# Reordering two stages of a four-layer graph network: deferred message sums in layer 2, blocks turned ahead in the front

## The chip, the cores and the metric

The kernel runs on one core of one Trainium2 chip. Its time is the device time of one launch in microseconds (us); the kernel before took 5975.33 us (median of 3 runs, 5974.05 to 5976.02). The profile comes from one further execution under the profiler, which took 6542.29 us by the clock and 6540.2 us from its first to its last instruction. So the profiled execution is longer than the timed ones, and numbers of the profile are used here to see which work waits for which, and how long single pieces take.

The engines are named as in the profile: PE (matmuls; PEld is its weight load), DVE (vector), ACT (scalar), POOL (which here issues the gathers), SP (which issues the plain DMAs). Each engine runs its own instructions in the order in which the program names them, so the order of the program text inside a loop is itself a tuning choice.

## The reference

Node features `x` are 4096 x 512, there are 65536 edges (`src`, `dst`, sorted by `dst`) with 64 attributes each. Four layers follow, each added to `x` after a layer norm and a relu. Cut to what matters here:

```python
# layer 0: attention. h = x W per head, scores of every edge, softmax over a node's edges
h = jnp.einsum('nc,hcf->hnf', x, W)
s_src = jnp.einsum('hnf,hf->hn', h, a_src); s_dst = jnp.einsum('hnf,hf->hn', h, a_dst)
...                                   # masked softmax over the adjacency, att @ h
# layer 1: agg @ weight, agg a degree-normed sum over edges
...
# layer 2: a message for every edge
edge_feat = jnp.concatenate([x[src], x[dst], edge_attr], axis=-1)
h = mish(edge_feat @ W1 + b1)
messages = mish(h @ W2 + b2)                                   # 65536 x 512
agg = jax.ops.segment_sum(messages, dst, num_segments=x.shape[0])
...                                   # two more products, a layer norm
# layer 3: a degree-normed sum over edges
```

`mish(x)` is `x * tanh(softplus(x))`.

## The kernel before

The edges are sorted on the chip (a bitonic sort of keys) and cut into tiles of 128 edges whose ends lie in one block of 128 nodes. A sum over a node's edges is then a matmul of a tile with a one-hot matrix of its places in the block, added to the accumulator `acc` of that block. Three parts of the kernel are concerned.

**Layer 2, the messages.** It handles 528 tiles in 132 groups of four (`U2 = 4`). The groups are software-pipelined: an iteration `i` does the second product of group `i-1`, the attribute product of group `i+1` and the sums of group `i-2`. A message tile is split into two float32r parts, so that a sum is two matmuls (`add_message`):

```python
def in_parts(m):
    parts = lp.tile([P, 2, 2, D], F32R, name="parts", bufs=2)
    nc.vector.tensor_copy(parts[:, 0], m)
    nc.vector.tensor_sub(parts[:, 1], m, parts[:, 0].bitcast(F32))
    return parts

def add_message(t, oh, parts):
    ps = lps.tile([P, D], F32, name="small_ps", bufs=4)
    for k in range(2):
        nc.tensor.matmul(ps, oh, parts[:, k], start=k == 0, stop=k == 1)
    add_to(block_of(nc.vector, bi_d, t), ps)          # DVE: acc[block] += ps

for i in range(-3, NG + 2):
    ...                                               # gathers of later groups (POOL)
    if now(i - 2):
        oh = one_hots(...)                            # DVE
        ...                                           # sigmoid of z (ACT)
    if now(i - 1):
        ps = second_product(h_t.pop(0))               # PE, 4 matmuls of 128x512
        nc.vector.tensor_add(zz[:, 0, :], ps, b2_bc)
    if now(i + 1):
        et = turn_attributes(...)                     # PE transposes, ACT copy
    if now(i - 1):
        h_t[2], h_t[3] = turn_h(2, hh), turn_h(3, hh)
    ...
    if now(i - 1):
        ps = second_product(h_t.pop(1))
        nc.vector.tensor_add(zz[:, 1, :], ps, b2_bc)
    if now(i + 1):
        made = attribute_products(et)                 # PE, 4
        ...                                           # 4 adds into pg (DVE)
    ...                                               # second_product 2 and 3
        nc.vector.tensor_mul(mz[:, :2], mz[:, :2], t[:, :2]); parts = [in_parts(mz[:, :2])]
    ...
        nc.vector.tensor_mul(mz[:, 2:], mz[:, 2:], t[:, 2:]); parts.append(in_parts(mz[:, 2:]))
    ...
    if now(i):
        for j in range(2): h_t[j] = turn_h(j, last)   # PE transposes, ACT copies
    if now(i - 2):
        for j in range(U2):
            add_message(..., oh[:, j, :], parts[j // 2][:, :, j % 2, :])
```

`parts`, `small_ps`, `tr_ps` (of the transposes) and `m_ps` (of the second product) are rings of 2, 4, 2 and 2 buffers; `oh` and `t` have one.

**The front: the product of layer 0.** For each of 32 blocks of 128 nodes, `project` normalizes (`hn`, DVE), turns (four transposes, PE; copy with relu, ACT), multiplies (four matmuls `wh_ps`, four narrow `s_ps`), and puts the block before away:

```python
for j in range(BG):
    ... # hn (DVE)
    yield
    h_t = relu_t(lp, lps, hn)         # PE transposes into tr, ACT relu to h_t
    if waiting is not None:
        put_away(*waiting)            # ACT copy, DVE copy, DMA to htab
    yield
    ps = lps.tile([P, D], F32, name="wh_ps")
    for k in range(KC):
        nc.tensor.matmul(ps, h_t[:, k, :], w_sb[:, k, :], ...)
        if k == 1: yield
    ... # s_ps: four matmuls of 128x16
    yield
```

Three generators take turns at their `yield`s: `project`, the sort `by_order(0)` (three of its steps to two turns), and `attributes` (DMAs).

**The end of a sort.** `placed` turns the sorted tiles (five groups of up to 128 tiles) so that a tile's edges lie along the partitions. It does so one group at a time through one PSUM buffer named `turn`; for `by_order(0)` it is called three times, for `by_order(1)`, beside the sums of layer 1, once:

```python
for g in range(G):
    n = min(P, TT - g * P)
    ps = ppool.tile([P, P], F32, name="turn")
    nc.tensor.transpose(ps, what[:, g, :], ident)
    nc.vector.tensor_copy(into[:, g * P:g * P + n], ps[:, :n])
```

Of the kernel before, what the change touches and what calls it, by code (L numbers as in the profile page):

```python
# [34 lines left out]
def kernel(  # L35
# [90 lines left out]
    def by_order(o, pool, ppool):  # L126
# [156 lines left out]

        def placed(into, what):

            for g in range(G):
                n = min(P, TT - g * P)
                ps = ppool.tile([P, P], F32, name="turn")
                nc.tensor.transpose(ps, what[:, g, :], ident)
                nc.vector.tensor_copy(into[:, g * P:g * P + n], ps[:, :n])  # L290

        blk_bc = blk.unsqueeze(2).to_broadcast([P, G, P])
        val = pool.tile([P, G, P], F32, name="val")
        if o == 1:
            nc.vector.scalar_tensor_tensor(val, blk_bc, float(-D_BLOCK), cur, op0=OP.mult, op1=OP.add)
            nc.vector.tensor_scalar(val, val, float(E), None, op0=OP.min)

            nc.vector.tensor_scalar(val, val, float(EA), odd, op0=OP.mult, op1=OP.add)
            yield
            placed(d_eid, val)  # L300
            return
        cur_i = pool.tile([P, G, P], I32, name="cur_i")
        nc.vector.tensor_copy(cur_i, cur)
        low = pool.tile([P, G, P], I32, name="low")
        nc.vector.tensor_scalar(low, cur_i, N - 1, None, op0=OP.bitwise_and)
        nc.vector.tensor_copy(val, low)
        placed(s_dst, val)
        nc.vector.tensor_scalar(cur_i, cur_i, 12, None, op0=OP.logical_shift_right)
        loc = pool.tile([P, G, P], F32, name="loc")
        nc.vector.tensor_copy(loc, cur_i)  # L310
        nc.vector.scalar_tensor_tensor(loc, blk_bc, float(-P), loc, op0=OP.mult, op1=OP.add)
        placed(s_loc, loc)

        new = pool.tile([P, G, P], F32, name="new")
        nc.vector.tensor_tensor(new, cur, prev, op=OP.not_equal)
        nc.vector.tensor_tensor(val, cur_i, low, op=OP.not_equal)
        nc.vector.tensor_mul(new, new, val)
        placed(s_new, new)
        yield

    def attributes(pool):
# [99 lines left out]
    def relu_t(pool, ppool, hn, relu=True):  # L421

        ps = ppool.tile([P, KC, P], F32, name="tr")
        for k in range(KC):
            nc.tensor.transpose(ps[:, k, :], hn[:, k * P:(k + 1) * P], ident)
        h_t = pool.tile([P, KC, P], F32, name="h_t")
        nc.scalar.activation(h_t, ps, AF.Relu if relu else AF.Copy)
        return h_t
# [16 lines left out]
    def one_hots(pool, loc, t0, n, bufs=None, ids=None, dtype=F32):  # L445

        oh = pool.tile([P, n, P], dtype, name="oh", bufs=bufs)
        nc.vector.tensor_tensor(oh, (row_i if ids is None else ids).unsqueeze(1).to_broadcast([P, n, P]),
                                loc[:, t0:t0 + n].unsqueeze(2).to_broadcast([P, n, P]), op=OP.is_equal)
        return oh  # L450
# [31 lines left out]
    def project(lp, lps):  # L482

        xs = {}

        def load(g):
            xs[g] = lp.tile([P, BG, D], F32, name="xt", bufs=3)
            nc.sync.dma_start(xs[g], blocks_of(x, g * BG))

        load(0)  # L490
        w_sb = lp.tile([P, KC, D], F32, name="w_sb", bufs=1)
        for h in range(H):
            nc.sync.dma_start(w_sb[:, :, h * F:(h + 1) * F], w0[h].rearrange("(k p) f -> p k f", p=P))
        wa = lp.tile([P, KC, 2, H], F32, name="wa", bufs=1)

        def weights_of_scores():
            for j in range(2):
                a_bc = lp.tile([P, H, F], F32, name="a_bc")
                nc.sync.dma_start(a_bc, a0[:, j * F:(j + 1) * F, 0].partition_broadcast(P))
                for k in range(KC):  # L500
                    t = lp.tile([P, H, F], F32, name="w_a")
                    nc.vector.tensor_mul(t, w_sb[:, k, :].rearrange("p (h f) -> p h f", h=H), a_bc)
                    nc.vector.reduce_sum(wa[:, k, j, :], t, axis=AX.X)
                    if k % 2:
                        yield

        class Later:


            def __init__(self, g):  # L510
                self.x = xs.pop(g)
                self.st = lp.tile([P, BG, 2], F32, name="st")
                self.rstd = lp.tile([P, BG], F32, name="rstd")
                self.root = lp.tile([P, BG], F32, name="root")

            def steps(self):
                var = self.st[:, :, 1]
                for j in range(BG):
                    stats(lp, self.st[:, j, :], self.x[:, j, :])
                    yield  # L520
                nc.vector.tensor_scalar(var, var, EPS, None, op0=OP.add)
                nc.scalar.activation(self.root, var, AF.Ln)
                nc.scalar.activation(self.rstd, self.root, AF.Exp, scale=-0.5)
                yield
                nc.vector.tensor_mul(self.root, self.rstd, self.rstd)
                nc.vector.tensor_mul(self.root, self.root, var)
                nc.vector.tensor_scalar(self.root, self.root, -0.5, 1.5, op0=OP.mult, op1=OP.add)
                nc.vector.tensor_mul(self.rstd, self.rstd, self.root)
                yield

        def put_away(b, ps, s_ps):
            nc.scalar.copy(acc[:, b, :D], ps)
            nc.vector.tensor_copy(node[:, b, 0:3:2, :], s_ps)
            nc.sync.dma_start(htab[b * P:(b + 1) * P, :D], acc[:, b, :D])

        groups = NB // BG
        norm = Later(0)
        load(1)
        yield from norm.steps()
        waiting = None  # L540
        for g in range(groups):
            if g + 2 < groups:
                load(g + 2)
            nxt = Later(g + 1) if g + 1 < groups else None
            ahead = nxt.steps() if nxt else iter(())
            for j in range(BG):
                hn = lp.tile([P, D], F32, name="hn")
                nc.vector.tensor_scalar(hn, norm.x[:, j, :], norm.st[:, j, 0:1], norm.rstd[:, j:j + 1],
                                        op0=OP.subtract, op1=OP.mult)
                next(ahead, None)  # L550
                yield
                h_t = relu_t(lp, lps, hn)
                if waiting is not None:
                    put_away(*waiting)
                yield
                ps = lps.tile([P, D], F32, name="wh_ps")
                for k in range(KC):
                    nc.tensor.matmul(ps, h_t[:, k, :], w_sb[:, k, :], start=k == 0, stop=k == KC - 1)
                    if k == 1:
                        yield  # L560
                if g == 0 and j == 0:
                    yield from weights_of_scores()
                s_ps = lps.tile([P, 2, H], F32, name="s_ps")
                for k in range(KC):
                    nc.tensor.matmul(s_ps.rearrange("p j h -> p (j h)"), h_t[:, k, :],
                                     wa[:, k].rearrange("p j h -> p (j h)"), start=k == 0, stop=k == KC - 1)
                waiting = g * BG + j, ps, s_ps
                if j % 2:
                    next(ahead, None)
                yield  # L570
            for _ in ahead:
                pass
            norm = nxt
        put_away(*waiting)

    with tc.tile_pool(name="sort", bufs=1) as sp, tc.tile_pool(name="sort_ps", bufs=1, space=PSUM) as spp, \
# [443 lines left out]
    with ExitStack() as l2:  # L1020
# [9 lines left out]
        def messages(ctx, first, last, fetched=None):  # L1030
# [53 lines left out]
            def second_product(h_t):  # L1084
                m_ps = lps.tile([P, D], F32, name="m_ps")
                product(m_ps, h_t, w2_sb)
                return m_ps
# [26 lines left out]


            fetched, rows, h, z, h_t = dict(fetched or {}), {}, {}, {}, {}
            pg = qg = None
            ctx.enter_context(tc.manual_schedule(engines=ENGINES))
            for i in range(-3, NG + 2):
                now = lambda k: 0 <= k < NG  # L1120
                if now(i + 2):
                    rows[i + 2] = fetch_rows(fetched[i + 2])
# [6 lines left out]
                if now(i) and i > 0:  # L1129
                    nc.scalar.activation(qg, qg, AF.Arctan)  # L1130
                if now(i - 2):
                    oh = one_hots(lp, d_loc, first + (i - 2) * U2, U2, bufs=1, dtype=F32R)
                    mz = z.pop(i - 2)
                    t = lp.tile([P, U2, D], F32, name="t", bufs=1)
                    nc.scalar.activation(t, mz, AF.Sigmoid, scale=-1.0)
                if now(i - 1):
                    hh = h.pop(i - 1)
                    zz = z[i - 1] = lp.tile([P, U2, D], F32, name="z", bufs=2)
                    ps = second_product(h_t.pop(0))
                    nc.vector.tensor_add(zz[:, 0, :], ps, b2_bc)  # L1140
                if now(i + 1):
                    et = turn_attributes(fetched[i + 1])
                    nxt = rows[i + 1]
                if now(i - 1):
                    h_t[2], h_t[3] = turn_h(2, hh), turn_h(3, hh)
                if now(i - 2):
                    nc.scalar.activation(t, t, AF.Arctan)
                if now(i + 1):
                    keep_ends(i + 1, fetched.pop(i + 1))
# [31 lines left out]
                    for j in range(2):  # L1181
                        h_t[j] = turn_h(j, last)
                if now(i - 2):
                    for j in range(U2):
                        add_message(first + (i - 2) * U2 + j, oh[:, j, :], parts[j // 2][:, :, j % 2, :])

        with tc.If(nc.values_load(more[:, 1:2], min_val=0, max_val=1) > 0):
            messages(TD_MAIN, TD)
# [220 lines left out]
```

## Time and profile before

| what | us |
|---|---|
| timed runs, median | 5975.33 |
| profiled execution, first to last instruction | 6540.2 |
| PE, DVE, ACT, POOL busy | 5567.4, 4364.9, 3086.2, 3919.6 |
| second product of layer 2: first and last start | 2384.1, 5122.1 |
| message sums of layer 2: first and last start | 2425.3, 5141.3 |
| front: first transpose of `project` | 24.2 |
| front: the last `node` copy of `project` | 265.65 |
| first gather of layer 0's attention | 275.98 |

The busy time of an engine over the whole span mixes stages with different limits; each of the changed stages is a stretch of its own in the trace (the front from 0 to about 270 us, the messages from about 2384 to 5144 us), and is read there. A line of the timeline gives the start, the time covered, the engine, the source line, the operation, what it writes and reads, the shape and the number of merged instructions; square brackets hold the idle time of that engine just before it and what ended it. float32 matmuls appear as two records each.

### The profile page before, as it was taken

The page shows a single profiled execution, that of the slowest core. Times are in us where ns is not written, and L with a number is a line of the kernel's source. Part 1 is how long each engine was busy: PE and PEld are TensorE (multiplying, and loading weights), DVE is VectorE, ACT ScalarE, POOL GpSimd, SP SyncE. Part 2 cuts the span into 40 slices and gives each one's busy share as a digit, 9 for nine tenths or more (in the row PEclk, how much of TensorE's full clock was granted, in tenths as well). Part 3 has the DMA queues.
Part 4 walks back from the last instruction along what each step waited for, and adds up shares of the span by engine and source line. Part 5 has one row for each costly group of instructions (what it writes and reads, how often), then busy time and mean ns, then how long its engine had stood idle before and what let it go on. Part 6 is the DMA issues. An engine that isn't in the chain of part 4 may idle for free. (4 is left out here: it accounts for less than half of the span.)

```text
span 6540.2 us, 65028 instructions
## 1 busy us (share of the span) xinstructions
PE 5567.4 (85%) x17918; PEld 2951.3 (45%) x17918; DVE 4364.9 (67%) x7420; ACT 3086.2 (47%) x4232; POOL 3919.6 (60%) x3326
## 2 busy tenths in 40 slices
PE   6576777688998869999999999999999899777777
PEld 4355555533443334444444444444444566422222
DVE  7466666755665448888888888888888555455555
ACT  3144444431110047777777777777777433100000
POOL 1255555316665658888888888888887111255664
PEclk9788888899999989999999999999999999877878
DMA  8655555456777745555555555555555111355665
GB/s 228 160 151 149 146 152 153 131 179 211 226 226 197 214 106 115 108 108 108 108 110 109 107 107 108 108 108 109 110 108 104 68 68 65 111 163 165 194 197 161
DMA packets 424659, 908.43 MB, mean 139 GB/s; under 512 B 135734, under 2 KB 135734, under 8 KB 424278
## 3 DMA queue, kind: packets, MB, share of 16 engines
q0 software_dynamic: 264768, 721.66, 44.6%
q1 hardware_dynamic: 159510, 182.40, 8.7%
q8 instruction: 153, 2.51, 0.2%
q14 instruction: 228, 1.87, 0.1%
HBM read 800.88 MB, written 102.94 MB: 138 GB/s over the span
## 5 line engine op out<-in xcount | busy, mean ns | idle before, releaser
L442 PE MATMUL m_ps<-w_sb,h_t 128*128 128x512 f32 x4224 | 1894.1, 596 | 3.2 <-ACT h_t L1081 3.0
L847 PE MATMUL sum_ps<-g,oh 128*128 128x512 f32 x2144 | 1152.5, 673 | 286.5 <-DVE acc L463 145.6
L442 PEld LDWEIGHTS m_ps<-w_sb,h_t 128*128 128x128 f32 x4224 | 781.9, 190 | 937.8 <-issue 922.9
L463 DVE TENSOR_TENSOR acc<-acc,sum_ps 128x512 f32 x800 | 550.0, 687 | 796.7 <-PE sum_ps L847 336.2
L1048 POOL DMA_INDIRECT pg<-qtab,eg x528 | 947.1, 1794 | 161.2 <-issue 160.6
L453 POOL DMA_INDIRECT pg<-ptab,eg x528 | 773.8, 1466 | 217.3 <-issue 160.3
L761 PE MATMUL sum_ps<-rows,oh 128*128 128x261 f32 x2176 | 619.3, 440 | 287.5 <-issue 197.6
L847 PEld LDWEIGHTS sum_ps<-g,oh 128*128 128x128 f32 x2144 | 429.1, 212 | 951.4 <-issue 574.1
L453 POOL DMA_INDIRECT g<-ytab,s_dst x544 | 544.7, 1001 | 491.3 <-DMA x_mid<-x 201.0
L453 POOL DMA_INDIRECT rows<-htab,s_dst x544 | 518.1, 952 | 482.1 <-PE sum_ps L761 285.6
L453 POOL DMA_INDIRECT g<-ztab,d_src x528 | 511.6, 969 | 409.5 <-PE sum_ps L847 173.2
L761 PEld LDWEIGHTS sum_ps<-rows,oh 128*128 128x128 f32 x2176 | 453.5, 217 | 391.8 <-issue 203.8
L988 POOL DMA_INDIRECT eg<-aug,d_eid x528 | 517.6, 980 | 160.9 <-issue 142.9
L1081 ACT COPY h_t<-tr_ps 128x512 f32<-128x512 f32 x528 | 296.3, 587 | 292.5 <-PE tr_ps L1079 271.7
L1349 ACT ACTIVATE t_end<-acc,dis 128x512 f32<-128x512 f32 x32 | 23.0, 722 | 847.9 <-DVE acc L463 806.4
L463 DVE TENSOR_TENSOR acc<-acc,small_ps 128x512 f32 x528 | 362.5, 687 | 80.2 <-DVE acc L463 60.6
L1099 PE MATMUL small_ps<-parts,oh 128*128 128x512 f32 x1056 | 314.9, 420 | 91.4 <-DVE parts L1093 80.7
L1156 DVE TENSOR_TENSOR pg<-pg,small_ps 128x512 f32<-128x512 f32 x528 | 328.3, 683 | 66.3 <-issue 38.6
L1152 DVE TENSOR_TENSOR z<-m_ps,b_bc 128x512 f32<-128x512 f32 x132 | 91.3, 692 | 376.7 <-PE m_ps L442 345.8
L1093 DVE TENSOR_TENSOR parts<-z,parts 128x1024 fp32r<-128x1024 f32 x264 | 323.4, 1225 | 9.0
L1079 PE MATMUL tr_ps<-ident,pg 128*128 128x128 f32 x2112 | 302.3, 276 | 5.4 <-DVE pg L1167 2.1
L768 DVE TENSOR_TENSOR acc<-acc,sum_ps 128x522 f32 x272 | 189.5, 697 | 173.7 <-PE sum_ps L761 159.6
(276 smaller groups left out, 8716.9 us busy)
## 6 DMA issues: line engine op xcount, KB each, us to landing
aug<-row SPq DMA_DIRECT2D x32, 560.0 KB
xt<-in_x_dram SPq DMA_DIRECT2D x16, 1024.0 KB
row<-in_edge_attr_dram SPq DMA_DIRECT2D x32, 512.0 KB
rows<-htab,s_dst POOLq DMA_INDIRECT x544
g<-ytab,s_dst POOLq DMA_INDIRECT x544
eg<-aug,d_eid POOLq DMA_INDIRECT x528
pg<-ptab,eg POOLq DMA_INDIRECT x528
pg<-qtab,eg POOLq DMA_INDIRECT x528
```

Of the source, the lines that this page charges most:

```text
L442: nc.tensor.matmul(ps, h_t[:, k, :], w_sb[:, k0 + k, :], start=start and k == 0, stop=stop and k == KC - 1)
L453: nc.gpsimd.indirect_dma_start(out=dst_ap, out_offset=None, in_=table, in_offset=bass.IndirectOffsetOnAxis(ap=idx, axis=0))
L463: nc.vector.tensor_add(into, into, ps)
L761: nc.tensor.matmul(ps[:, c, :HW], oh[:, j + k, :], rows[:, j + k, c * HW:(c + 1) * HW], start=k == 0, stop=k == 1)
L847: nc.tensor.matmul(ps, oh[:, j + k, :], g[:, j + k, :], start=k == 0, stop=k == pair - 1)
L988: nc.gpsimd.indirect_dma_start(out=eg[:, j // 2, (j % 2) * HALF:(j % 2 + 1) * HALF], out_offset=None, in_=aug.rearrange("e c -> (e c)").un ...
L1048: nc.gpsimd.indirect_dma_start(out=pg[:, j, :], out_offset=None, in_=qtab, in_offset=bass.IndirectOffsetOnAxis(ap=end_of(eg, j, 1), axis=0 ...
L1079: nc.tensor.transpose(h_ps[:, k, :], h[:, j, k * P:(k + 1) * P], ident)
L1081: nc.scalar.copy(h_t, h_ps)
L1093: nc.vector.tensor_sub(parts[:, 1], m, parts[:, 0].bitcast(F32))
L1099: nc.tensor.matmul(ps, oh, parts[:, k], start=k == 0, stop=k == 1)
L1156: nc.vector.tensor_add(nxt[:, j], nxt[:, j], made[j])
```

## The change

In layer 2 only the first two of a group's four sums stay at the end of the iteration. The other two are kept in a list `left` and issued in the next iteration, right behind the first `second_product` and ahead of its `zz` addition; the one-hots of the next group move behind them, since `oh` has one buffer. This is meant to give the second `in_parts` of the group time to end before PE comes to the sums that read it. The loop runs one iteration longer, for the last group's two sums.

In the front the normalized blocks come from a generator `norms()`, and the block `b+1` is turned between the two halves of the product of block `b`, so that PE has matmuls to do while ACT copies the turned block. And `placed` turns four groups into one PSUM tile and takes them away with one copy, with a `yield` between the transposes and the copy.

```diff
         def placed(into, what):
-            for g in range(G):
-                n = min(P, TT - g * P)
-                ps = ppool.tile([P, P], F32, name="turn")
-                nc.tensor.transpose(ps, what[:, g, :], ident)
-                nc.vector.tensor_copy(into[:, g * P:g * P + n], ps[:, :n])
+            for g in range(0, G, 4):
+                n = min(4, G - g)
+                ps = ppool.tile([P, n, P], F32, name="turn")
+                for k in range(n):
+                    nc.tensor.transpose(ps[:, k, :], what[:, g + k, :], ident)
+                yield
+                cols = slice(g * P, min((g + n) * P, TT))
+                nc.vector.tensor_copy(into[:, cols], ps.rearrange("p g t -> p (g t)")[:, :cols.stop - cols.start])
 ... (placed(...) becomes yield from placed(...), four times)
 ... (project; norms() makes the hn, with the same steps of the next norm between)
-                h_t = relu_t(lp, lps, hn)
-                if waiting is not None:
-                    put_away(*waiting)
-                yield
-                ps = lps.tile([P, D], F32, name="wh_ps")
-                for k in range(KC):
-                    nc.tensor.matmul(ps, h_t[:, k, :], w_sb[:, k, :], start=k == 0, stop=k == KC - 1)
-                    if k == 1:
-                        yield
+        for b in range(NB):
+            ps = lps.tile([P, D], F32, name="wh_ps")
+            for k in range(KC // 2):
+                nc.tensor.matmul(ps, h_t[:, k, :], w_sb[:, k, :], start=k == 0, stop=False)
+            yield
+            h_next = relu_t(lp, lps, hn) if b + 1 < NB else None
+            if waiting is not None:
+                put_away(*waiting)
+            yield
+            for k in range(KC // 2, KC):
+                nc.tensor.matmul(ps, h_t[:, k, :], w_sb[:, k, :], start=False, stop=k == KC - 1)
+            hn = next(made, None)
+            yield
 ... (the narrow products s_ps as before; then h_t = h_next)
 ... (layer 2)
-            for i in range(-3, NG + 2):
+            for i in range(-3, NG + 3):
 ...
                 if now(i - 2):
-                    oh = one_hots(lp, d_loc, first + (i - 2) * U2, U2, bufs=1, dtype=F32R)
                     mz = z.pop(i - 2)
 ...
                     ps = second_product(h_t.pop(0))
+                while left:
+                    add_message(*left.pop(0))
+                if now(i - 1):
                     nc.vector.tensor_add(zz[:, 0, :], ps, b2_bc)
 ...
                 if now(i - 2):
+                    oh = one_hots(lp, d_loc, first + (i - 2) * U2, U2, bufs=1, dtype=F32R)
                     nc.scalar.activation(t, t, AF.Arctan)
 ...
                 if now(i - 2):
-                    for j in range(U2):
-                        add_message(first + (i - 2) * U2 + j, oh[:, j, :], parts[j // 2][:, :, j % 2, :])
+                    left = [(first + (i - 2) * U2 + j, oh[:, j, :], parts[j // 2][:, :, j % 2, :]) for j in range(U2)]
+                    for j in range(2):
+                        add_message(*left.pop(0))
```

More of the change, by code (lines that the diff above doesn't have):

```diff
@@ L299, in by_order @@
             yield
-            placed(d_eid, val)
+            yield from placed(d_eid, val)
             return
@@ L306, in by_order @@
         nc.vector.tensor_copy(val, low)
-        placed(s_dst, val)
+        yield from placed(s_dst, val)
         nc.vector.tensor_scalar(cur_i, cur_i, 12, None, op0=OP.logical_shift_right)
@@ L311, in by_order @@
         nc.vector.scalar_tensor_tensor(loc, blk_bc, float(-P), loc, op0=OP.mult, op1=OP.add)
-        placed(s_loc, loc)
+        yield from placed(s_loc, loc)
         new = pool.tile([P, G, P], F32, name="new")
@@ L317, in by_order @@
         nc.vector.tensor_mul(new, new, val)
-        placed(s_new, new)
+        yield from placed(s_new, new)
         yield
@@ L534, in put_away @@
             nc.sync.dma_start(htab[b * P:(b + 1) * P, :D], acc[:, b, :D])
[L536 to L539, printed above, removed]
-        waiting = None
[L541 to L550, printed above, removed]
-                yield
-                h_t = relu_t(lp, lps, hn)
-                if waiting is not None:
-                    put_away(*waiting)
-                yield
-                ps = lps.tile([P, D], F32, name="wh_ps")
-                for k in range(KC):
-                    nc.tensor.matmul(ps, h_t[:, k, :], w_sb[:, k, :], start=k == 0, stop=k == KC - 1)
-                    if k == 1:
[L560 to L573, printed above, removed]
@@ new lines, in norms @@
+        def norms():
+            norm = Later(0)
+            load(1)
+            for _ in norm.steps():
+                yield None
+            for g in range(NB // BG):
+                if g + 2 < NB // BG:
+                    load(g + 2)
+                nxt = Later(g + 1) if g + 1 < NB // BG else None
+                ahead = nxt.steps() if nxt else iter(())
+                for j in range(BG):
+                    hn = lp.tile([P, D], F32, name="hn")
+                    nc.vector.tensor_scalar(hn, norm.x[:, j, :], norm.st[:, j, 0:1], norm.rstd[:, j:j + 1],
+                                            op0=OP.subtract, op1=OP.mult)
+                    next(ahead, None)
+                    if j % 2:
+                        next(ahead, None)
+                    yield hn
+                for _ in ahead:
+                    pass
+                norm = nxt
@@ new lines, in project @@
+        made = norms()
+        for hn in made:
+            if hn is not None:
+                break
+            yield
+        h_t = relu_t(lp, lps, hn)
+        hn = next(made)
+        yield
+        waiting = None
+        for b in range(NB):
[6 more added lines that the diff above has]
+                put_away(*waiting)
+            yield
+            for k in range(KC // 2, KC):
+                nc.tensor.matmul(ps, h_t[:, k, :], w_sb[:, k, :], start=False, stop=k == KC - 1)
+            hn = next(made, None)
+            yield
+            if b == 0:
+                yield from weights_of_scores()
+            s_ps = lps.tile([P, 2, H], F32, name="s_ps")
+            for k in range(KC):
+                nc.tensor.matmul(s_ps.rearrange("p j h -> p (j h)"), h_t[:, k, :],
+                                 wa[:, k].rearrange("p j h -> p (j h)"), start=k == 0, stop=k == KC - 1)
+            waiting = b, ps, s_ps
+            h_t = h_next
+            yield
@@ L1116, in messages @@
             fetched, rows, h, z, h_t = dict(fetched or {}), {}, {}, {}, {}
-            pg = qg = None
+            pg, qg, left = None, None, []
             ctx.enter_context(tc.manual_schedule(engines=ENGINES))
-            for i in range(-3, NG + 2):
+            for i in range(-3, NG + 3):
                 now = lambda k: 0 <= k < NG
```

## The prediction

> **What bounds the kernel now.** I read the page's 40 slices first, for the stages, and then each changed stage by itself.
>
> ```profile
> PE   6576777688998869999999999999999899777777
> PEclk9788888899999989999999999999999999877878
> ```
>
> The messages of layer 2 (2384 to 5144 us) are the long row of nines: PE is nearly full there, at full clock. The table of windows says how full:
>
> ```profile
> 3400.00:3900.00 500.00, 484.86 (x1589) 239.56 (x1587) 405.29 (x555) 394.16 (x313) 411.96 (x289) 1.00 0.53 108
> ```
>
> Columns: window; busy time of PE, PEld, DVE, ACT, POOL; granted clock; DMA share; GB/s. PE is idle for 15.1 of 500 us. One group lasts 20.78 us (the record that starts at 3600.58 comes again at 3621.36), so PE idles 15.1 x 20.78 / 500 = 0.63 us a group. The timeline of PE over one group shows where:
>
> ```profile
> 3600.58 1.99 PE L1072 MATMUL small_ps<-w1e,et 64*128 64x512 f32 x8
> 3602.50 7.13 PE L442 MATMUL m_ps<-w_sb,h_t 128*128 128x512 f32 x16
> 3609.47 1.04 PE L1079 MATMUL tr_ps<-ident,pg 128*128 128x128 f32 x8
> 3610.26 1.39 PE L1099 MATMUL small_ps<-parts,oh 128*128 128x512 f32 x5
> 3612.26 0.96 PE L1099 MATMUL small_ps<-parts,oh 128*128 128x512 f32 x3 [0.61 <-DVE parts L1093]
> 3613.06 3.60 PE L442 MATMUL m_ps<-w_sb,h_t 128*128 128x512 f32 x8
> 3616.50 0.38 PE L1062 MATMUL tr_ps<-ident,eg 128*128 128x128 f32 x2
> 3616.72 1.28 PE L1079 MATMUL tr_ps<-ident,pg 128*128 128x128 f32 x8
> 3617.83 3.60 PE L442 MATMUL m_ps<-w_sb,h_t 128*128 128x512 f32 x8
> ```
>
> Of the eight sum matmuls five run, then PE stands 0.61 us until the group's second split (`parts`, L1093) is done. The list of waits from 2500 to 5000 us (sum, times, longest) says that this is PE's only wait, and that DVE's longest is for PE:
>
> ```profile
> PE small_ps L1099 <- DVE parts L1093: 72.6, 120, 0.6
> DVE z L1152 <- PE m_ps L442: 314.6, 110, 2.9
> ```
>
> The two make a closed loop. Product 1 ends; DVE adds it at once (3600.69) and then works with next to no break up to the end of the second split (10.98 + 1.23 = 3612.21); PE does the last three sum matmuls, product 0, transposes, product 1 again:
>
> ```profile
> 3600.69 0.69 DVE L1152 TENSOR_TENSOR z<-m_ps,b_bc 128x512 f32<-128x512 f32 x1 [2.91 <-PE m_ps L442]
> ...
> 3610.98 1.23 DVE L1093 TENSOR_TENSOR parts<-z,parts 128x1024 fp32r<-128x1024 f32 x1
> ```
>
> For the front: PE's timeline, and its waits from 53 to 262 us. One block, and the end of the sort:
>
> ```profile
> 59.24 0.63 PE L425 MATMUL tr<-ident,hn 128*128 128x128 f32 x4
> 60.56 3.70 PE L558 MATMUL wh_ps<-w_sb,h_t 128*128 128x512 f32 x8 [0.69 <-ACT h_t L427]
> 64.09 0.96 PE L565 MATMUL s_ps<-wa,h_t 128*128 128x16 f32 x8
> ...
> 234.10 0.33 PE L289 MATMUL turn<-ident,val 128*128 128x128 f32 x1 [0.39 <-DVE s_dst L290]
> ```
>
> ```profile
> PE wh_ps L558 <- ACT h_t L427: 20.8, 28, 1.1
> ```
>
> Every block costs PE about 0.7 us of waiting for its own turned copy, 20.8 us in all; at the end PE and DVE hand one small buffer back and forth.
>
> **What the Trainium skill says.** "Perfetto Trace Analysis", section "Tensor Engine Instruction (MATMUL, LD_WEIGHTS)": the end of a matmul record is estimated from its size, its start is observed. The trace agrees: 3602.50 + 7.13 overlaps the next start at 3609.47. So I count from start to start. "SBUF — State Buffer", section "Who interferes with whom": a DVE instruction in a two-port mode, or with two SBUF inputs against a reading GpSimd, shuts GpSimd out. The trace fits: the gather-adds that POOL issues take 1.54 to 1.58 us beside an idle DVE and up to 2.46 us beside L1161, whose inputs are both in SBUF. "TensorE: Matmul & The Clock Gate", section "Why this matters for your kernels": gaps over about 3 us lower the clock. The gap of 0.61 us does not: the window shows 1.00. So only the gap itself is to be won in layer 2. "VectorE: DVE Perf Modes", section "The TRN2 errata": a fixed cost per instruction, so one large copy is cheaper than four small ones. Four copies of 128x128 from `turn` take 4 x 0.29 = 1.16 us here; a DVE read of 128x512 from PSUM takes 0.68 (the z additions).
>
> **The change, part by part.**
>
> *Layer 2, what is removed.* No instruction is added or dropped; two sums (four matmuls, two DVE additions) move behind product 0. Start to start, sum matmuls without a wait cost (3613.06 - 3612.26) / 3 = 0.27 us each, so eight cost 2.13. Now they take 3613.06 - 3610.26 = 2.80. The difference is 0.67; I take off 0.06 for one more change between kinds of matmul (product 0 to sums), which leaves 0.61 us, the gap that PE shows.
>
> *Layer 2, does the wait come back elsewhere?* Let attributes start at 0. PE: attributes to 1.92, products 2 and 3 to 8.89, transposes to 9.68, two sums to 10.75, product 0 to 14.2, two sums to 15.3, transposes to 16.6, product 1 to 20.15. DVE's second split ends at 11.6, so the moved sums find it 2.6 us old. Product 0 needs the first turned copy: ACT's copies begin 0.64 after the transposes and take 0.58 each, so it is there at 10.1 against a need at 10.75. DVE does the first two additions by 14.8, the moved two from 15.0 to 16.6, then z 0, the one-hots and the small copies (0.6 + 0.6 + 0.5) to about 18.3, and is free for product 1 at 20.15. The 2.9 us for which DVE waits now shrink to about 1.9 and stay positive. `m_ps` for product 2 is freed at 17.2, long before its start. Every ring of buffers holds. So a group becomes about 20.78 - 0.61 = 20.17 us, and 131 steady groups save 131 x 0.61 = 80 us. The additional iteration holds two sums only: nothing.
>
> *Front, blocks turned ahead.* 28 waits of about 0.7 vanish from PE, 20.8 us. But the front isn't PE's alone: in the windows from 80 to 200 us DVE is busy 28 to 31 of 40 us, and the sort goes DVE to PE to ACT to DVE at each of 14 turns, with about 2 us of pure passage (71.18 the first turn on PE, ACT's copy at 72.4 for 0.58). That chain costs about 100 + 28 us of the same 134 us (71 to 205), so I credit about half, 10 us. At the start the second block no longer waits for its own normalizing (2.1 us at 44.86) and turning: 3 us.
>
> *Front, the end.* By the order of instructions in the two built programs, 2.75 blocks of the product stood behind the last `placed` (249.2 to 265.65: 16.4 us). In the changed one, one block and a half stand there: 3 halves of `wh_ps` at 1.8, two `s_ps` at 0.8, one turn at 0.6, 7.6 us. The `placed` stretch itself (233.4 to 249.7) loses about 1.3 us at each of three calls, for fewer hand-overs, but gets project's pieces put between: unchanged. 8 us saved.
>
> *Layer 1.* The other sort's `placed` holds PE and DVE for 4 us (2070 to 2074); about 2 saved.
>
> The sum is 80 + 10 + 3 + 8 + 2 = 103 us: 5975 - 103 = 5872. I take layer 2's part over from the profile one to one, since at clock 1.00 PE can't have been faster unprofiled.
>
> **The rivals.**
>
> *POOL takes over in layer 2.* For: its 12 gathers of a group take 17.13 us and stand 12 times 0.30 apart, 20.77 of 20.78 us: it never rests. If that were its own pace, the group would stay at 20.78 and only the front's 23 us be won: 5952. Against: at the stage's start its groups took 18.85, 19.27 and 19.53 us (gather-adds beginning at 2388.60, 2407.45, 2426.72, 2446.25), since then other gathers lay beside DVE's blocking work; and in the steady part nobody waits for a landing gather. Its length adapts to DVE's pace, down to 20.2 as well. I give it 1 in 15.
>
> *DVE takes over, or a new wait on the turned copy.* DVE has 16.84 us busy of 20.17, and its slack of 1.9 us would have to be off by 2. If product 0 waited for ACT, half the gain would go: 5910. 1 in 12.
>
> *DMA bounds the front.* From 80 to 200 us the DMA share is 0.78 to 0.83 at 209 to 222 GB/s, and reached 1.02 at 259 in the first 40. A front shorter by 8% asks for about 235: it fits, but the loads of the edge attributes may take some of the gain. Then 5885.
>
> *All of the front is PE's.* Then 20 instead of 10 us: 5860; with 0.67 us a group, 88 in layer 2, 5853, just over 2%.
>
> **Range and chances.** The centre is 5872, a gain of 1.7%. Layer 2 can hardly give over 88 nor, if it works, under 65; the front 5 to 33. The 8-in-10 range is 5848 to 5905. Over 2% means below 5855.8, which needs both parts at their upper ends: 0.19. Slower by over 2% would need a stall of more than 1.5 us in every group: 0.01. Within 2%: 0.80.
>
> **What would show it.** Right: a layer 2 group of 20.1 to 20.25 us; no PE wait for `parts`; PE idle under 0.1 us a group; DVE's wait for product 1 down to about 2 us; POOL's gathers of a group 17.1 to 16.5 us. In the front no PE wait for `h_t`, and the first attention gather at 249 to 268 us instead of 275.98. Wrong: a PE wait for `h_t` (L1081) before product 0, a DVE wait for a landing gather before the pg additions, or waits of PE for `key` in the front that replace those for `h_t`.

## The result, and the profile after

| | before | after |
|---|---|---|
| median of the timed runs, us | 5975.68 | 5844.02 |
| lowest to highest of four, us | 5974.05 to 5981.1 | 5842.2 to 5850.29 |

The ratio is 0.978, with a 95% interval of 0.9763 to 0.9797. The change saves 131.7 us; the prediction had 103, and its range reached to 127 (5975 - 5848).

In the profile that the prediction read (6540.2 us) attention and layer 1 took 2128.5 us and what follows the messages 1415.2, against 1747.3 and 1230.4 in a second profile of the same kernel; the messages took 2720.5 against 2721.4. Four of the runs below (all four sums, one sum, and each part of the front alone) are from a chip where the kernel before takes 6523.35 us (median). That the first profile came from a chip of that kind fits, but is not on record. Every run is therefore compared with the kernel before on its own chip, and the stages below with the second profile of the kernel before (5974.8 us), which is as long as the timed runs.

| stage (profiled) | before, us | after, us | difference |
|---|---|---|---|
| front, to the first gather of attention | 275.75 | 261.05 | -14.7 |
| attention of layer 0 and layer 1, to the first group's last `z` addition in layer 2 | 1747.3 | 1743.3 | -4.0 |
| messages of layer 2, to the last `z` addition | 2721.4 | 2607.8 | -113.6 |
| all that follows | 1230.4 | 1230.0 | -0.4 |
| span | 5974.8 | 5842.1 | -132.7 |

Between the first and the last `z` addition of that source line lie 131 groups: 20.77 us each before, 19.91 after. So a group lost 0.86 us where the prediction had 0.61, and this is where most of the surplus is.

The 40 slices of the page after, first PE's busy tenths, then the granted clock:

```profile
PE   6788887799999799999999999999999899988877
PEclk9899999999999899999999999999999999999999
```

The nines of layer 2 look like before; tenths don't resolve a gain of 4%. The table of windows does, with the columns of the prediction. First the kernel after, its whole message stage and a window in its middle:

```profile
2004.00:4612.00 2608.00, 2600.64 (x8624) 1312.85 (x8622) 2187.96 (x2996) 2140.77 (x1696) 2081.00 (x1538) 1.00 0.54 111
2900.00:3400.00 500.00, 499.36 (x1663) 252.40 (x1661) 421.51 (x578) 410.59 (x326) 408.26 (x302) 1.00 0.55 113
```

and the kernel before, its whole message stage:

```profile
2023.00:4744.00 2721.00, 2635.82 (x8623) 1304.12 (x8623) 2195.21 (x2996) 2140.76 (x1697) 2185.07 (x1539) 1.00 0.53 106
```

PE is now idle for 0.64 of 500 us, against 15.1 before. The reader should also see what doesn't add up: over the stage the idle time fell from 85.2 to 7.4 us, by 78, but the stage became 113 us shorter. The other 35 us came out of PE's *busy* time (2635.82 to 2600.64), with the same count of records and the same clock. Busy time of PE thus held some 35 us in which it did nothing.

One group on PE after the change (timeline, columns as in the prediction):

```profile
3399.14 1.04 PE L1099 MATMUL tr_ps<-ident,pg 128*128 128x128 f32 x8
3399.93 1.18 PE L1119 MATMUL small_ps<-parts,oh 128*128 128x512 f32 x4
3400.95 3.60 PE L445 MATMUL m_ps<-w_sb,h_t 128*128 128x512 f32 x8
3403.98 1.48 PE L1119 MATMUL small_ps<-parts,oh 128*128 128x512 f32 x4
3405.30 0.38 PE L1082 MATMUL tr_ps<-ident,eg 128*128 128x128 f32 x2
...
3406.64 3.60 PE L445 MATMUL m_ps<-w_sb,h_t 128*128 128x512 f32 x8
3410.17 1.99 PE L1092 MATMUL small_ps<-w1e,et 64*128 64x512 f32 x8
3412.09 7.13 PE L445 MATMUL m_ps<-w_sb,h_t 128*128 128x512 f32 x16
3419.06 1.04 PE L1099 MATMUL tr_ps<-ident,pg 128*128 128x128 f32 x8
```

(The sums, line 1099 before, are line 1119 here.) No line has a bracket: four sum matmuls, product 0 (the group's first `second_product`), the moved four, and PE waits for nobody. From transposes to transposes it is 3419.06 - 3399.14 = 19.92 us. DVE and POOL follow. DVE's wait for product 1, and POOL's twelve gathers (four of `qtab` with addition, four of `ptab`, four of `aug`) from one group to the next:

```profile
3410.28 0.69 DVE L1175 TENSOR_TENSOR z<-m_ps,b_bc 128x512 f32<-128x512 f32 x1 [1.97 <-PE m_ps L445]
```

```profile
3398.78 2.54 POOL L1068 DMA_INDIRECT pg<-qtab,eg  x1 [0.30 <-issue]
3401.62 1.67 POOL L1068 DMA_INDIRECT pg<-qtab,eg  x1 [0.30 <-issue]
...
3416.09 2.29 POOL L1068 DMA_INDIRECT pg<-qtab,eg  x1 [0.30 <-issue]
3418.68 2.54 POOL L1068 DMA_INDIRECT pg<-qtab,eg  x1 [0.30 <-issue]
```

DVE's slack shrank to 1.97 us and stayed positive. POOL still never rests, yet its twelve gathers now take 16.26 us (17.13 before), which with twelve gaps of 0.30 is again the whole period.

### The profile page after: what moved, and what is told of

Its sections match the earlier page's. It is cut to its first block, busy times and chain, and to the rows that moved or that the text cites. A ratio compares the mean times of both kernels' runs of the same rounds, so it can differ in the third digit from the quotient of the medians.

```text
span 5842.1 us, 65009 instructions
## 1 busy us (share of the span) xinstructions
PE 5318.2 (91%) x17918; PEld 2821.0 (48%) x17918; DVE 4349.0 (74%) x7408; ACT 3083.9 (53%) x4232; POOL 3819.1 (65%) x3326
## 5 line engine op out<-in xcount | busy, mean ns | idle before, releaser
L867 PE MATMUL sum_ps<-g,oh 128*128 128x512 f32 x2144 | 1074.8, 618 | 155.7 <-DMA g<-ztab,d_src 94.5
L1068 POOL DMA_INDIRECT pg<-qtab,eg x528 | 1038.9, 1968 | 161.1 <-issue 159.2
L867 PEld LDWEIGHTS sum_ps<-g,oh 128*128 128x128 f32 x2144 | 377.8, 193 | 792.6 <-DVE acc L466 341.2
L1008 POOL DMA_INDIRECT eg<-aug,d_eid x528 | 565.5, 1071 | 161.0 <-issue 146.6
L456 POOL DMA_INDIRECT pg<-ptab,eg x528 | 530.5, 1005 | 205.4 <-issue 160.0
L781 PE MATMUL sum_ps<-rows,oh 128*128 128x261 f32 x2176 | 529.6, 391 | 111.5 <-issue 103.3
L781 PEld LDWEIGHTS sum_ps<-rows,oh 128*128 128x128 f32 x2176 | 399.5, 191 | 194.5 <-issue 128.9
L1119 PE MATMUL small_ps<-parts,oh 128*128 128x512 f32 x1056 | 353.4, 456 | 12.4 <-DVE parts L1112 10.7
L1290 POOL TENSOR_TENSOR h_sb<-h_sb,b_bc 128x1024 f32<-128x1024 f32 x16 | 37.7, 2359 | 435.7 <-PE tr L1274 357.9
L1099 PEld LDWEIGHTS tr_ps<-ident,pg 128*128 128x128 f32 x2112 | 239.9, 141 | 108.7 <-issue 54.9
```

Of the source, the lines that this page charges most:

```text
L456: nc.gpsimd.indirect_dma_start(out=dst_ap, out_offset=None, in_=table, in_offset=bass.IndirectOffsetOnAxis(ap=idx, axis=0))
L781: nc.tensor.matmul(ps[:, c, :HW], oh[:, j + k, :], rows[:, j + k, c * HW:(c + 1) * HW], start=k == 0, stop=k == 1)
L867: nc.tensor.matmul(ps, oh[:, j + k, :], g[:, j + k, :], start=k == 0, stop=k == pair - 1)
L1008: nc.gpsimd.indirect_dma_start(out=eg[:, j // 2, (j % 2) * HALF:(j % 2 + 1) * HALF], out_offset=None, in_=aug.rearrange("e c -> (e c)").un ...
L1068: nc.gpsimd.indirect_dma_start(out=pg[:, j, :], out_offset=None, in_=qtab, in_offset=bass.IndirectOffsetOnAxis(ap=end_of(eg, j, 1), axis=0 ...
L1099: nc.tensor.transpose(h_ps[:, k, :], h[:, j, k * P:(k + 1) * P], ident)
```

## The experiments

Three explanations of the surplus stood against each other: that the hole in PE is really larger than the record shows (A); that the front gave more (B); that the new order of PE's work gains something of its own (C).

**The kernel before, once more.** No edit.

> The kernel before, unchanged, for one more profile: the first profile lasted 6540 us where the timed runs take 5975. Expected: about 5975 us, a layer 2 group of 20.78 us as in the first profile (that stage ran at full clock there), and the excess of the first profile found in the gather stages outside layer 2.

It took 5976.88 us. Its profile is the column "before" of the stages above. The front's first gather stood at 275.75, so the front gave 14.7 us, less than the 21 predicted for it (10 + 3 + 8): the surplus is not there, and B falls. The first gather is only a landmark of the front; the run with the front alone, below, says the same of the time.

**Layer 2 alone.** The kernel before with only the layer 2 part of the diff above.

> Only the layer 2 part of the change; the front and placed as before. Theory A (the hole behind the wait was 0.86 us a group, deeper than the 0.61 that the record shows): group 19.9 us, 131 x 0.86 = 113 us saved, 5863 us. Rival B (the wait was worth 0.61 as predicted, and the rest of the gain is from the front): 5895 us.

5869.1 us against 5978.66 on this chip, ratio 0.9812 (0.9795 to 0.9828), 109.6 us less. A group takes (4639.0 - 2028.4) / 131 = 19.93 us. The saving of layer 2 is whole without the front.

**The wait taken away, the order kept.** The kernel before, in which the last two sums read the first split. It leaves out the sums of the second half of each group (the first half is summed twice); the second split is still computed, but PE doesn't need it.

```diff
-    add_message(..., oh[:, j, :], parts[j // 2][:, :, j % 2, :])
+    add_message(..., oh[:, j, :], parts[0][:, :, j % 2, :])
```

> The kernel before with its old order, but the last two sums of a group read the first split instead of the second: the sums of the second half of each group are left out and those of the first half are added to their blocks instead. So the wait is gone and nothing is moved. Theory A (the gain is the whole hole, hidden behind modelled matmul ends): group 19.9 to 20.0 us, about 5865 us. Rival C (0.61 us is the wait, and 0.25 us is won by the new order, in which product 0 and the sums follow one another more tightly): group 20.17, 5895 us.

5865.02 us against 5978.66, ratio 0.9807 (0.979 to 0.9823); a group takes (4632.7 - 2024.2) / 131 = 19.91 us, as in the changed kernel. With the order of before and no wait, the whole gain is there: C falls. PE's timeline of this kernel gives the eight sums back to back:

```profile
3400.90 2.10 PE L1099 MATMUL small_ps<-parts,oh 128*128 128x512 f32 x8
3402.84 3.60 PE L442 MATMUL m_ps<-w_sb,h_t 128*128 128x512 f32 x8
3406.27 0.38 PE L1062 MATMUL tr_ps<-ident,eg 128*128 128x128 f32 x2
```

Start to start that is 3402.84 - 3400.90 = 1.94 us, or 0.2425 for one. The kernel before, on the same kind of chip, at the same place:

```profile
3417.26 1.39 PE L1099 MATMUL small_ps<-parts,oh 128*128 128x512 f32 x5
3419.25 0.96 PE L1099 MATMUL small_ps<-parts,oh 128*128 128x512 f32 x3 [0.60 <-DVE parts L1093]
3420.05 1.45 PE L442 MATMUL m_ps<-w_sb,h_t 128*128 128x512 f32 x3
```

3420.05 - 3417.26 = 2.79 us. The difference, 0.85 to 0.86 us, is what the wait costs. Five sums fill 5 x 0.2425 = 1.21 us of the 1.99 between the first and the sixth start, so PE stood 0.78; the last three then take 0.80 instead of 0.73, a restart of 0.07. The record shows 0.60 of it, because it lets the fifth matmul end 0.18 us later than the next could have begun. Over 131 groups 0.18 + 0.07 make 33 us, which is about what went missing from PE's busy time. A holds. That the hole cost 0.86 us is shown by the two runs without it; its division into 0.18 and 0.07 is worked out from the starts.

**Four sums behind, or one.** The change moves two. Moving all four leaves nothing between the transposes and product 0, moving one leaves PE at the second split again.

```diff
-                    for j in range(2):
+                    for j in range(3):      # only the last sum is moved
                         add_message(*left.pop(0))
```

For four, the two lines are taken out. Otherwise both are the kernel with layer 2 alone.

> Layer 2 part alone, with all four sums put behind the next group's first product. Then product 0 follows directly on the transposes of its own operand. Theory A (the two sums left in place are a cover for ACT's copy, which ends 1.2 to 1.3 us after the transposes start, while PE is done with them after 0.8): a wait of PE for h_t of about 0.5 us a group, 60 to 70 us slower than the layer 2 part alone, about 5928 us. Rival (product 0 finds its operand ready): as the layer 2 part alone, 5863 us.

6474.5 us against 6523.35 on this chip, ratio 0.9921 (0.9898 to 0.9943); a group takes (5073.6 - 2400.3) / 131 = 20.41 us, 0.48 more than with two (19.93, measured on another chip; with layer 2 untouched a group takes 20.77 us on both). PE's timeline shows what the two sums left in place are good for:

```profile
3707.54 1.04 PE L1079 MATMUL tr_ps<-ident,pg 128*128 128x128 f32 x8
3708.82 3.70 PE L442 MATMUL m_ps<-w_sb,h_t 128*128 128x512 f32 x8 [0.24 <-ACT h_t L1081]
3711.96 2.41 PE L1099 MATMUL small_ps<-parts,oh 128*128 128x512 f32 x8
```

Product 0 now waits for ACT's turned copy: the rival of the prediction, seen when it is let in. Here too the record (0.24) is less than the loss (0.48): from the transposes to the next start are 3708.82 - 3707.54 = 1.28 us, where the changed kernel shows 3399.93 - 3399.14 = 0.79.

> Layer 2 part alone, with only the last sum put behind the next group's first product. The third sum still waits at its second matmul for the second split. Theory A (the loop from product 1 over DVE to the third sum and back sets the group's time): nothing won but the two matmuls of the fourth sum that now lie outside the wait's shadow, which stay in the same loop: within 10 us of the kernel before, 5970 us. Rival (gain in proportion to the sums moved): half of 113 us, 5919 us.

6521.22 (median of 19) against 6523.35 us, ratio 0.9993 (0.9982 to 1.0004), with a twentieth execution of 13949.62 us left out as a slow one whose cause is unknown; a group takes (5115.2 - 2390.9) / 131 = 20.80 us. Nothing is gained:

```profile
3704.58 1.40 PE L1099 MATMUL small_ps<-parts,oh 128*128 128x512 f32 x5
3706.58 0.50 PE L1099 MATMUL small_ps<-parts,oh 128*128 128x512 f32 x1 [0.60 <-DVE parts L1093]
3706.92 3.59 PE L442 MATMUL m_ps<-w_sb,h_t 128*128 128x512 f32 x8
```

The same hole stands ahead of the sixth matmul. The loop from product 1 over DVE back to PE still closes through one sum matmul that reads the second split, and while one does, the loop's length is the group's.

**The front: both parts, and each alone.** The kernel before with the new front; then with the blocks turned ahead alone, and with four tiles at a time in `placed` alone.

> Only the front's part and placed; layer 2 as before. Theory A: the front's 15 us (end of project 265.65 to 250.30 in the two profiles) and 1 to 3 us in layer 1: 5958 us. Rival B (the front and layer 1 give more than the traces of two unlike executions show, about 50 us): 5925 us.

5960.59 us against 5978.66, ratio 0.997 (0.9957 to 0.9982), 18 us less; the first gather at 261.7, the layer 2 group unchanged at 20.76.

> Only the blocks turned ahead in the front; placed and layer 2 as before. Theory A (the sort's chain over DVE, PE and ACT takes over from PE in the front; the sort ends about 7 us earlier, and the tail behind it shrinks by fewer blocks): 8 to 12 us saved, 5965 us. Rival (PE's 21 us of waits all come back): 5955 us.

6517.1 against 6523.35 us, ratio 0.9986 (0.9973 to 0.9999), 6 us less; the first gather at 270.7.

> Only placed with four tiles at a time; project and layer 2 as before. Theory A: 2 to 8 us saved, 5970 us, most of it in the front's tail, where pieces of the product now lie between the hand-overs. Rival (the added turns of the generators cost as much as the fewer hand-overs save): 5975 us.

6508.18 against 6523.35 us, ratio 0.9974 (0.9955 to 0.9993), 15 us less; the first gather at 271.5. The intervals of these two reach from under 1 to nearly 18 us and from under 5 to 29, too wide to tell which part gave more. In kernels whose front is untouched that gather stood between 274.9 and 283.7 us, so single profiles here are good to some us only. The landmarks inside the front say more (PE's `turn<-signs`, with which the search after the sort begins, and the last `node` copy of `project`; us from the start):

| | first turn of keys | `turn<-signs` | last `node` copy | first to second | second to third |
|---|---|---|---|---|---|
| before | 71.4 | 210.9 | 265.4 | 139.5 | 54.5 |
| after | 75.4 | 203.7 | 250.3 | 128.3 | 46.6 |
| turned ahead alone | 76.2 | 201.9 | 260.4 | 125.7 | 58.5 |
| four at a time alone | 72.0 | 211.6 | 261.0 | 139.6 | 49.4 |

Turning ahead shortens the sort (first to second) and four tiles at a time the end (second to third). The sort is untouched by the second part (139.6); the end is 4.0 us longer with the first part alone (58.5), in one profile each.

**What holds the front now.** The list of waits of the kernel after from 28 to 262 us (sum, times, longest) has no wait for `h_t` on PE, which was 23.0 us in 31 before. Others stand in its place: the three for `wa`, `key` and `val` below were 8.8, 0.8 and 3.0 us in the kernel before, and are 18.8 us longer together.

```profile
PE s_ps L589 <- DVE wa L506: 12.9, 4, 9.2
...
PE turn L177 <- DVE key L168: 10.3, 5, 5.7
...
DVE cur_i L306 <- DMA win<-line,off_i: 8.3, 1, 8.3
PE turn L290 <- DVE val L309: 8.2, 1, 8.2
```

The last two lines are one wait: the sort waits for the gathers `win`. It gives up five turns there, and when these are used up DVE stands at the next instruction of the sort and PE behind it, though `project` still has work. Three kernels were run beside the changed one again: more turns for the others, the product `w_a` (from which `wa` is made at the start) taken from DVE to POOL, and both.

> The changed kernel unchanged, beside its two variants on one chip. Expected: ratio 0.978 to the kernel before where that takes 5975 us; where it takes about 6520, the same 132 us less.

5850.76 us (5847.75 to 5852.31) against 5984.84, ratio 0.9778 (0.9764 to 0.9791).

```diff
-        for _ in range(5):
+        for _ in range(11):
             yield
```

> The changed kernel with 11 instead of 5 turns between the sort's gathers of its sorted keys and their first use, so that one more block of the product lies in PE's 8.2 us of waiting for them. Theory A (the front's tail is a chain of hand-overs, and what stands behind it counts in full): the first attention gather 4 to 5 us earlier than in the changed kernel (261.05 us in its profile), 0.1% of the time. Rival (the block in the wait delays the hand-overs by as much): no change in the first gather.

5836.5 us (5831.91 to 5843.01), ratio 0.9755 (0.9742 to 0.9769): 14.3 us less than the changed kernel on the same chip, whose runs it doesn't overlap, and the fastest of the study. The wait shrank, in the list of waits of this kernel over the same stretch:

```profile
PE turn L290 <- DVE val L309: 2.1, 1, 2.1
```

The last `node` copy came at 241.8 instead of 250.3, the first gather at 252.65, 8.2 us earlier than in the changed kernel (260.88); 4 to 5 were expected. The other 6 us of the time have no cause that was shown. The same lines serve the second sort, beside layer 1, too, so the edit acts there as well; the stretch from the first gather to the messages took 1745.9 us against 1749.3 in the changed kernel beside it, but that stretch lies between 1733.8 and 1750 in profiles of this study.

```diff
-                    nc.vector.tensor_mul(t, w_sb[:, k, :].rearrange(...), a_bc)
+                    nc.gpsimd.tensor_mul(t, w_sb[:, k, :].rearrange(...), a_bc)
```

> The changed kernel with the eight products w_a of the front (128x512 each, 0.68 us on DVE) on POOL. Theory A (with the blocks turned ahead DVE and the sort bound the front's first 75 us: PE waits 9.2 us for wa and 5.7 us for key there): the first turn of keys on PE (75.39 us in the changed kernel's profile) comes 3 to 5 us earlier, and so does the first attention gather. Rival (PE still bounds the front): the first turn moves, the first gather doesn't.

5851.03 us, ratio 0.9777 (0.9764 to 0.9791): no gain, and the first gather came 7 us later (267.9). The timelines of POOL and of DVE in this kernel show how:

```profile
39.72 0.59 POOL L343 COPY row<-three 128x48 int32<-128x48 int32 x2
45.70 5.11 POOL L505 TENSOR_TENSOR w_a<-w_sb,a_bc 128x512 f32<-128x512 f32 x4 [5.39 <-DMA a_bc<-in_L_gnn_a_dram]
```

```profile
46.99 0.69 DVE L506 TENSOR_REDUCE wa<-w_a 128x8 f32<-128x512 f32 x1 [4.23 <-POOL w_a L505]
```

One product takes POOL 5.11 / 4 = 1.28 us where DVE took 0.68, DVE stood 4.23 us for it, and PE's longest wait for `wa` grew to 13.0 us. But POOL itself stood 5.39 us here, for the second load of `a_bc`. SP issued that load at 40.72 us, against 29.57 in the changed kernel beside it: ahead of it in SP's order stands the store of the edge rows into `aug`, which needs POOL's copies (`row<-three`, 39.72), and these now stand behind the first products on POOL. DVE was relieved of work, but the chain through POOL and SP became longer. The time did not follow the landmark, though: it is that of the changed kernel (5850.76). In the profiles the stretch from the first gather to the messages was 6.2 us shorter (1743.1 against 1749.3); no run shows why.

> Both front variants together. Theory A: their gains add, the first attention gather 7 to 10 us earlier than in the changed kernel, about 0.15% off its time, 5835 us where the changed kernel takes 5844.

5842.52 us, ratio 0.9768 (0.9755 to 0.9782): 8.2 of the 14.3 us are left. The gains don't add, as had been expected (5835). The first gather stands at 261.7, no earlier than in the changed kernel; in the profiles the gain lies behind it, where the same stretch took 1733.8 us, and has no cause that was shown.

## Why the prediction was off, point by point

*Layer 2, what is removed: the step that failed, by its size.* The mechanism held: the wait for the second split goes, nothing takes its place. But the term "0.27 us each, so eight cost 2.13 ... the difference is 0.67; I take off 0.06 ... which leaves 0.61" measured 0.86. Two things in it were wrong. The 0.27 came from the three sums right behind the wait, which contain the restart; undisturbed sums take 0.2425, eight 1.94. And the 0.06 for one more change between kinds of matmul doesn't exist: in the changed kernel sums, product 0 and sums take 1.02 + 3.03 + 1.32 = 5.37 us (3399.93 to 3405.30), and without the wait in the old order 1.94 + 3.43 = 5.37 (3400.90 to 3406.27). What confirmed the wrong figure was that it met the idle time on record. The Trainium skill's "Perfetto Trace Analysis", section "Tensor Engine Instruction (MATMUL, LD_WEIGHTS)", had been cited: ends are estimated, starts observed. The prediction did count from start to start, but it took its pitch from behind the wait and then let the idle time on record confirm the rest, and an idle time begins at an estimated end. The runs agree with the page, and add a size: 0.60 on record for 0.86 of cost. 131 x 0.86 = 113 us instead of 80.

*The wait elsewhere.* Right. DVE's slack was put at about 1.9 and is 1.97; product 0 has its turned copy in time, as long as two sums stand before it (moving four shows the margin).

*POOL takes over.* Rightly put aside: the twelve gathers were to shrink from 17.1 to 16.5 us, and shrank to 16.26, with the period.

*Blocks turned ahead, 10 us.* Right in size: the sort's stretch lost 139.5 - 128.3 = 11.2, about half of PE's 20.8 us of waits. "About half" was a guess, so this is luck in part: a block on PE undisturbed by the sort fell from 5.67 us (54.94 to 60.61 in the timeline before) to 4.77 (84.50 to 89.27 after), 0.9 each, which over 31 blocks would be 28 us. One sign of being wrong came true here: PE waits for `key` 10.3 us in the front where it waited 0.8.

*The start, 3 us saved.* Wrong in sign: the first turn of keys came 4.0 us later. PE's timeline, first of the kernel after, then of before:

```profile
41.55 0.61 PE L589 MATMUL s_ps<-wa,h_t 128*128 128x16 f32 x2 [9.24 <-DVE wa L506]
...
75.39 2.08 PE L177 MATMUL turn<-turns,key 128*128 128x128 f32 x8 [5.74 <-DVE key L168]
```

```profile
38.38 0.61 PE L565 MATMUL s_ps<-wa,h_t 128*128 128x16 f32 x2 [6.00 <-DVE wa L503]
...
71.36 1.16 PE L177 MATMUL turn<-turns,key 128*128 128x128 f32 x8 [0.58 <-DVE key L168]
```

In the changed kernel DVE normalizes further ahead, and in its order this stands before `wa` and before the first keys; the block that was ready early only gave PE a longer wait. That the additional work on DVE is the cause is read from these two waits; no run took it away.

*The end, 8.* Right, and by the mechanism named: 54.5 - 46.6 = 7.9 us, and from the last `turn<-ident,new` to the last `node` copy are 250.3 - 242.7 = 7.6 us, the predicted figure, against 265.4 - 249.2 = 16.2 before. *DMA bounds the front:* not seen. From 80 to 120 us the changed kernel moved 236 GB/s at a DMA share of 0.86, what the prediction asked for (235). *Layer 1, 2 us:* not resolved; the stage was 4.0 us shorter (1743.3), but took 1749.3 us in the second profile of the changed kernel, as in kernels with the layer unchanged (1747.3 to 1750).

In the sum, -113.6 and -14.7 stand for -80 and -21: the under-measured hole gave 33 us more, the front 6 less. The upper rival, "0.67 us a group, 88 in layer 2", was still short of it. (Its sums are off by one or two: 5975 - 113 is 5862, not 5860, and 5975 - 121 is 5854, not 5853; nothing rests on it.)

## What to carry to other kernels

Measure a hole in PE by the distance between the starts around it, less the undisturbed pitch of the same matmuls found elsewhere, and not by the idle time on record; if the pitch can only be had from matmuls behind the wait, it contains the restart. Before trusting a gain worked out from idle time, look whether "busy" at the same place is longer than the same instructions take elsewhere. When work is put behind other work, leave enough in place to cover the next engine's latency, and move all that closes the loop: here two sums of four were right, one gained nothing and four gave more than half back.

## What the hardware showed

A sum matmul (128x512, both operands f32r) is issued every 0.2425 us, while the last of five has 0.42 on record (1.39 - 4 x 0.2425): its estimated end lies 0.18 us behind the moment at which the next could start. One more change from sums to the f32 product and back cost nothing that could be measured (5.37 against 5.37 us). POOL's twelve gathers fitted the group in both kernels: they took 17.13 us in a group of 20.78 and 16.26 in one of 19.9, so an engine without a pause need not be the bound. And an f32 product of 128x512 took POOL 1.28 us, nearly twice DVE's 0.68. One copy of 128x512 from `turn` took DVE 0.69 us, where four of 128x128 had taken 4 x 0.29 = 1.16.
